# Graph layers on one core: three VectorE operands moved forward in order, and two pairs of column-sum products joined

## The chip, the core and the metric

The kernel runs on one core of a Trainium2 chip. The metric is the device time of one execution in microseconds (us); the time before is the median of three runs. One further execution was recorded by the hardware profiler, and everything about single instructions comes from that one. Engines are called TensorE (PE in the profile; PEld is its weight load), VectorE (DVE), ScalarE (ACT), GpSimd (POOL) and SyncE (SP, which issues transfers here). All data is fp32.

## The reference

For each of 16 graphs there are a feature matrix x (1024 nodes x 128) and an adjacency matrix adj (1024 x 1024). What matters of it:

```python
# first network, then a residual and a layer norm
degree = adj.sum(axis=-1)[:, :, None]
s = einsum('bid,bij->bjd', x, adj) / degree
x = layernorm(x + relu(concat([x, s]) @ W.T + b))

# second network: four layers, then a residual and a layer norm
def layer(nodes, ws, bs, wd, bd, wn, bn, wu, bu):
    src = einsum('bjv,bij->biv', nodes @ ws + bs, adj / norm_of_rows(adj))
    dst = einsum('bjv,bji->biv', nodes @ wd + bd, adj / norm_of_columns(adj))
    own = nodes @ wn + bn
    return tanh(concat([src, own, dst]) @ wu + bu)
# layers three and four read earlier outputs beside the last one
```

So each graph needs the Euclidean norms of the rows and of the columns of adj, row sums (degrees), and two layer norms over 128 features.

## The kernel before

**Loop.** The program runs over the 16 graphs, `for b in range(B)`. Within a step it does layers one to four of the second network for graph b and, in the gaps of the other engines, prepares graph n = b + 1: it loads adj, takes sums and norms, scales rows and columns, runs the first network (`first_gnn`, between layers three and four) and its layer norm (during layer four). The layer norm that ends graph b - 1 is done during layer two of graph b. The source counts layers from 0: l = 0, 1, 2, 3 are layers one to four.

**Order.** The order on each engine is written by hand (`manual_schedule`): instructions stand on an engine as the Python code issues them. A layer's matrix products come from lists; `aggregate` walks them and calls `hooks[i]` ahead of the i-th product of the upper list. These hooks place the other engines' work, and the small products, among the large ones.

**Halves.** A product fills 64 of the 128 columns of the TensorE array, so two run at the same time, one for the upper and one for the lower 64 output rows (`flat_steps`, `in_turn`). TensorE takes its instructions in order, alternating between the halves. Each fp32 product stands in the trace as two records.

**A layer.** `messages` or, for layers three and four, `paired_messages` computes what nodes send: TensorE writes into PSUM banks (tag `pt`, four buffers used in turn), VectorE adds the bias and writes the tiles t. `message_sums` makes from them the operands of a seven-product scheme (in place of eight): S3 = X00 - X10, S1 = X10 + X11, S2 = S1 - X00, S4 = X01 - S2, each with a SRC and a DST part. On the other side stand combinations of the adjacency (T, Q). In layers three and four the nodes' own features go through the same scheme, with T2, T3, T4 made in `begin_paired`, `t3()` and `t4()`. `aggregate` then runs the products M1 to M4 and Z11 to Z21 and adds their results up through the tiles e0, e1 and e2; `m2_and_half_of_m3` (line 906) is one of those reads, and it issues the addition of line 908.

**Sums over partitions.** VectorE reduces along the free axis. What is left across partition groups is summed on TensorE by `sum_groups` (line 247): two products with the constant `fold`, one per half, 32 columns wide. Six such sums are taken per graph: `pc` in `inverses` (column norms, layer two), `pm` in `norm_centre` and `pv` in `norm_rstd` (mean and variance of the layer norm, once in layer two and once in layer four), and `rp` in `gather_inverses` (row factors, layer three). Powers of -0.5 are taken on GpSimd (lines 374 and 454).

The changed places, by lines of before: column sums 340 to 343, `inverses` 360 to 370, `row_inverses` and `gather_inverses` 376 to 389, `norm_sum` and `norm_centre` 423 to 439, `messages` and `message_sums` 684 to 712, `begin_paired` and `paired_messages` 714 to 823, `aggregate` from 906 on, and the hooks of layers two, three and four.

Of the kernel before, what the change touches and what calls it, by code (L numbers as in the profile page):

```python
# [8 lines left out]
F32 = mybir.dt.float32  # L9
# [5 lines left out]
P = 128  # L15
# [8 lines left out]
def adj_resnorm_kernel(ctx: ExitStack, tc: tile.TileContext, x, adj, w0, b0, layers, out):  # L24
# [118 lines left out]
    def message_seven(wm):  # L143
        return seven(wm, (wm, MSUMS), 2 * P, P)
# [94 lines left out]
    def small(name, shape=(K,)):  # L239
        return ps_s.tile([P, *shape], F32, tag="small", name=name)  # L240
# [6 lines left out]
    def sum_groups(out, y):  # L247

        for s in (slice(V, P), slice(V)):
            nc.tensor.matmul(out[s], fold, y, start=True, stop=True)  # L250
# [89 lines left out]
    def column_reduce(b, state, tr):  # L340
        part = two.tile([P, K], F32, tag="part", name=f"part{b}")
        nc.vector.reduce_sum(part, tr.rearrange("p (k r) -> p k r", r=C), axis=AX.X)
        state["part"] = part
# [15 lines left out]

    def inverses(b, state, first=0):  # L360

        cols = state["cols"]
        pc = small(f"pc{b}")
        sum_groups(pc, state["part"])
        own = one.tile([P, NH, G, BPH], F32, tag="own", name=f"own{b}")
        nc.vector.tensor_mul(own, pc.rearrange("p (h g k) -> p h g k", h=NH, g=G),
                             group[:, None, :, None].to_broadcast([P, NH, G, BPH]))
        nc.vector.reduce_sum(cols[:, NB:2 * NB].rearrange("p (h k) -> p h k", h=NH),
                             own.rearrange("p h g k -> p h k g"), axis=AX.X)
        root_inverses(cols, state["inv"], slice(first, 2 * NB))  # L370
# [4 lines left out]

    def row_inverses(b, inv):

        spread = one.tile([P, NH, G, BPH], F32, tag="own", name=f"sp{b}")
        nc.vector.tensor_mul(spread, inv[:, :NB].rearrange("p (h k) -> p h k", h=NH)[:, :, None, :]
                             .to_broadcast([P, NH, G, BPH]),  # L380
                             group[:, None, :, None].to_broadcast([P, NH, G, BPH]))
        return spread
# [39 lines left out]

    def norm_sum(ys, ks, name, xs=None):

        if xs is not None:
            nc.vector.tensor_add(ys[:, ks], ys[:, ks], xs[:, ks])
        s = two.tile([P, ks.stop - ks.start], F32, tag="part", name=f"s{name}")
        nc.vector.reduce_sum(s, ys[:, ks], axis=AX.X)
        return s

    def norm_centre(ys, s, ks, name):
        n = ks.stop - ks.start
        pm = small(f"pm{name}")
        sum_groups(pm[:, :n], s)
        nc.vector.scalar_tensor_tensor(ys[:, ks], pm[:, :n, None].to_broadcast([P, n, C]), -1.0 / D,
                                       ys[:, ks], op0=ALU.mult, op1=ALU.add)
        sq = two.tile([P, n, C], F32, tag="sq", name=f"sq{name}")
        nc.scalar.activation(sq, ys[:, ks], AF.Square)
        return sq
# [244 lines left out]
    def messages(b, l, feats, wm, between={}, with_sums=True):  # L684


        nch = CHUNKS[l]
        t = [one.tile([P, NJ, 2, 2, V], F32, tag=f"t{j}", name=f"t{l + 1}_{b}_{j}") for j in range(2)]
        for n, g in enumerate((2, 3, 0, 1)):
            pt = ps_t.tile([P, 2, 2 * P], F32, tag="pt", name=f"pt{l + 1}_{b}_{g}")  # L690
            for q in range(2):
                i = 2 * g + q
                for k, (f, c) in enumerate(feats):
                    by_halves(pt[:, q], f[:, i * P:(i + 1) * P], wm[:, 1 + c], k == 0, k == nch - 1)
            j, o = divmod(2 * g, NJ)
            nc.vector.tensor_add(t[j][:, o:o + 2].rearrange("p k a v c -> p k (a v c)"), pt,
                                 wm[:, 0][:, None, :].to_broadcast([P, 2, 2 * P]))
            if n in between:
                between[n]()
        return message_sums(b, l, t) if with_sums else t  # L700

    def message_sums(b, l, t):

        S = {i: one.tile([P, NJ, 2, V], F32, tag=f"S{i}", name=f"S{i}_{l + 1}_{b}") for i in (2, 3, 4)}
        X = {(v, j): t[j][:, :, :, v] for v in range(2) for j in range(2)}
        S[1] = X[1, 0]
        for part in (DST, SRC):
            nc.vector.tensor_sub(S[3][:, :, part], X[0, 0][:, :, part], X[1, 0][:, :, part])
        nc.vector.tensor_add(S[1], X[1, 0], X[1, 1])  # L709
        nc.vector.tensor_sub(S[2], S[1], X[0, 0])  # L710
        nc.vector.tensor_sub(S[4], X[0, 1], S[2])
        return X, S

    def begin_paired(b, l, first, second, etag):

        e12 = one.tile([P, 2, HW], F32, tag=etag, name=f"e12_{l}_{b}")
        y = {(j, h): f[:, half(h)] for j, f in enumerate((first, second)) for h in range(NH)}
        w = {"e12": e12, "y": y, "T2": e12[:, 1], "T4": e12[:, 0]}
        nc.vector.tensor_sub(w["T2"], y[1, 1], y[0, 1])
        return w  # L720

    def paired_messages(b, l, w, wm, rest=None, between={}):

        t = [one.tile([P, NJ, 2, 2, V], F32, tag=f"t{j}", name=f"t{l + 1}_{b}_{j}") for j in range(2)]
        X = {(v, j): t[j][:, :, :, v] for v in range(2) for j in range(2)}
        y, s, T2, T4 = w["y"], message_seven(wm), w["T2"], w["T4"]
        T3 = w["e0"] = one.tile([P, HW], F32, tag="e0", name=f"e0_{l}_{b}")
        o = own_seven(l, wm)
# [41 lines left out]
        if l == 2:  # L770
            at(0)
            m4 = into(bank(4), (y[0, 1], s["S1"]))
            nc.scalar.copy(X[1, 1], parts(m4))
            m1 = into(bank(1), (y[0, 0], s["w00"]))
            add_bias((0, 0), parts(m1), 0)
            t3()
            t4()
# [15 lines left out]
        else:  # L793
# [25 lines left out]
            at(4)  # L819
        XS = message_sums(b, l, t)  # L820
        if l == 2:
            at(3)
        return XS

# [27 lines left out]
    def aggregate(b, l, feats, msgs, wm, a, at, T, Q, fT, etag, hooks={}, pieces=1, w=None):  # L852
# [50 lines left out]
        def m3_half():  # L903
            nc.scalar.copy(e1[high], Dk[low])

        def m2_and_half_of_m3():
            m2_read()
            nc.vector.tensor_add(e0[high], e0[high], e1[high])

# [24 lines left out]
        elif l == 1:  # L934
# [15 lines left out]

            events = {10: first_reads, 14: m4_read, 18: m2_and_half_of_m3, 22: last_reads}
        else:
# [303 lines left out]
    at = [transposed(0, h) for h in range(NH)]  # L1256
    back = None

    for b in range(B):
# [142 lines left out]
        else:  # L1404
# [3 lines left out]
            if nxt:  # L1408
                sums_of_next = {0: sums_of(4, 5), 1: sums_of(of=FIRST, add=(4, 5)), 2: sums_of(6, 7),
                                8: sums_of(add=(6, 7)), 9: lambda: column_sums(n, st), 15: sums_of(of=(4,)),  # L1410
                                18: sums_of(of=(5,)), 20: lambda: inverses(n, st), 21: sums_of(of=(6,)),
                                24: sums_of(of=(7,))}

            def begin1(w=w, nm=nm):
                norm_spread(w["ys"], f4, KS)
                w["s"] = norm_sum(w["ys"], KS, nm, back)

            def centre1(w=w, nm=nm):
                w["sq"] = norm_centre(w["ys"], w["s"], KS, nm)
                if nxt:  # L1420
                    w["xs"] = load_spread(n)

            def squares1(w=w, nm=nm):
# [4 lines left out]

            hooks = alongside(sums_of_next, {2: begin1, 16: centre1, 19: squares1, 26: rstd1})
        hooks = alongside(hooks, {3: weights2})  # L1430
# [39 lines left out]
        def factors_of_rows(w=w):  # L1470
            w["spread"] = row_inverses(n, st["inv"])

        def factors_gathered(w=w):
            w["rinv"] = gather_inverses(n, w["spread"])

# [14 lines left out]
        if nxt:  # L1490
            scales = [lambda: scale(0, 1), lambda: scale(NJ, 1), lambda: scale(0, 0), lambda: scale(NJ, 0)]
            if b == 0:
                between = {1: inverses3, 2: factors}
                hooks = {1: load_xn, 5: factors_of_rows, 7: start3, 18: factors_gathered,
                         **dict(zip((10, 12, 14, 16), scales))}
                quarters_at = (20, 22, 25)
            else:
                between = {0: factors, 3: end1_and_load}
                hooks = {2: factors_of_rows, **dict(zip((4, 5, 7, 9), scales)), 10: factors_gathered, 16: start3}
                quarters_at = (12, 14, 25)  # L1500
            hooks |= dict(zip(quarters_at, (quarter1, x_sums, quarter2)))
# [11 lines left out]
        if nxt:  # L1513
            yT = first_gnn(n, w["X"], w["xT"], quarters(a2), w["T2"], w["dinv"])
            rinv = w["rinv"]

# [4 lines left out]
        if nxt:  # L1521
# [19 lines left out]

            def sum0(w=w):
                w["s"] = norm_sum(w["ys"], KS, nm)

            def centre0(w=w):
                w["sq"] = norm_centre(w["ys"], w["s"], KS, nm)

# [141 lines left out]
```

## Time and profile before

| what | value |
|---|---|
| median of three runs | 2396.12 us (2395.91 to 2396.41) |
| the profiled execution, its own time | 2395.86 us |
| its span, first to last instruction | 2394.1 us |
| mean granted TensorE clock | 0.999 of full speed |
| records of TensorE products with 32 columns | 368, that is 92 sums: pm 30, pv 30, pc 16, rp 16 |
| one graph, from pv of layer two to the next (552.07 to 698.51 us) | 146.44 us |
| VectorE busy in such a stretch (702.1 to 848.6 us) | 131.85 us |
| ScalarE busy in it | 61.27 us |

The page gives busy time by engine, the share of the span in 40 slices, the chain of work that ended last, and groups of equal instructions by line. A line such as `L1003 PE MATMUL m<-a,t 128*64 128x512 f32` is an instruction of line 1003 of the kernel that writes tile m from tiles a and t, with 64 columns of the array and 512 columns of data. In a timeline a row has its start, how long it took, what it is, how many equal ones were merged (x), and in brackets the idle time ahead of it. Ends of TensorE products are modelled; starts are recorded.

### The profile page before, as it was taken

The page shows a single profiled execution, that of the slowest core. Times are in us where ns is not written, and L with a number is a line of the kernel's source. Part 1 is how long each engine was busy: PE and PEld are TensorE (multiplying, and loading weights), DVE is VectorE, ACT ScalarE, POOL GpSimd, SP SyncE. Part 2 cuts the span into 40 slices and gives each one's busy share as a digit, 9 for nine tenths or more (in the row PEclk, how much of TensorE's full clock was granted, in tenths as well). Part 3 has the DMA queues.
Part 4 walks back from the last instruction along what each step waited for, and adds up shares of the span by engine and source line. Part 5 has one row for each costly group of instructions (what it writes and reads, how often), then busy time and mean ns, then how long its engine had stood idle before and what let it go on. Part 6 is the DMA issues. An engine that isn't in the chain of part 4 may idle for free.

```text
span 2394.1 us, 39329 instructions
## 1 busy us (share of the span) xinstructions
PE 2377.4 (99%) x15289; PEld 1279.6 (53%) x15289; DVE 2092.6 (87%) x2817; ACT 980.8 (41%) x1845; POOL 275.8 (12%) x103
## 2 busy tenths in 40 slices
PE   8999999999999999999999999999999999999998
PEld 4444564645556455554655546456464554645555
DVE  6998888999889989889988889888898988998954
ACT  5425345253343524435244452434525344352322
POOL 4101111001111011110111110111100111101110
PEclk9999999999999999999999999999999999999999
DMA  9527244262533627335272442634427253362400
GB/s 205 124 75 147 69 115 90 70 148 57 135 78 81 138 48 157 61 97 115 55 163 55 108 97 71 147 69 110 91 70 151 57 133 76 80 141 48 100 22 22
DMA packets 363387, 232.03 MB, mean 97 GB/s; under 512 B 150353, under 2 KB 334306, under 8 KB 363202
## 3 DMA queue, kind: packets, MB, share of 16 engines
q1 hardware_dynamic: 362386, 227.03, 42.5%
q0 software_dynamic: 816, 2.49, 0.4%
q8 instruction: 121, 1.98, 0.4%
q14 instruction: 64, 0.52, 0.1%
HBM read 209.59 MB, written 19.84 MB: 96 GB/s over the span
## 4 chain that ended last, share of the span: by engine, by line
PE 92%; DVE 1%; issue 0%; POOLq 0%; ACT 0%; DVEq 0%
PE m L1003 40%; PE z L1003 28%; PE pt L245 9%; PE pt_z L245 5%; PE m_f L581 5%; PE z_f L581 2%; PE pw L245 2%; PE m3s L1003 1%; PE pt_p L245 1%; DVE t L752 0%; PE pv L250 0%; PE pm L250 0%; DVE f L534 0%; PE rp L250 0%; DVE t L758 0%
## 5 line engine op out<-in xcount | busy, mean ns | idle before, releaser
L1003 PE MATMUL m<-a,t 128*64 128x512 f32 x1008 | 434.7, 593 | 0.2 <-DVE t L709 0.2
L1003 PE MATMUL m<-at,t 128*64 128x512 f32 x1008 | 418.6, 592 | 0.0
L1003 PE MATMUL m<-Q,S 128*64 128x512 f32 x880 | 394.0, 593 | 0.0
L1003 PE MATMUL m<-T,S 128*64 128x512 f32 (+1 forms) x1040 | 393.6, 573 | 0.0
L454 POOL TENSOR_TENSOR rs<-ve,mhalf 128x32 f32<-128x32 f32 x30 | 191.9, 6396 | 988.4 <-DVE ve L452 988.4
L1003 PE MATMUL z<-at,t 128*64 128x512 f32 x504 | 229.2, 592 | 0.0
L1003 PE MATMUL z<-at,S 128*64 128x512 f32 x504 | 228.3, 593 | 0.0
L1003 PE MATMUL z<-a,S 128*64 128x512 f32 x504 | 228.2, 593 | 0.0
L1003 PE MATMUL z<-a,t 128*64 128x512 f32 x504 | 227.2, 593 | 0.0
L1003 PE MATMUL z<-Q,t 128*64 128x512 f32 x504 | 227.0, 593 | 0.0
L1003 PEld LDWEIGHTS m<-T,S 128*64 128x64 f32 x1040 | 131.3, 137 | 129.5 <-issue 127.6
L1003 PEld LDWEIGHTS m<-Q,S 128*64 128x64 f32 x880 | 118.2, 137 | 150.4 <-issue 143.0
L1003 PEld LDWEIGHTS m<-at,t 128*64 128x64 f32 x1008 | 131.6, 137 | 110.7 <-issue 109.4
L1003 PEld LDWEIGHTS m<-a,t 128*64 128x64 f32 x1008 | 132.0, 137 | 109.8 <-issue 101.0
L1003 PE MATMUL z<-T,t 128*64 128x512 f32 x384 | 172.8, 592 | 0.0
L882 ACT COPY e<-m 64x512 f32<-64x512 f32 x63 | 36.7, 582 | 327.4 <-PE m L1003 327.0
L374 POOL TENSOR_TENSOR inv<-cols,mhalf 128x16 f32<-128x16 f32 (+1 forms) x17 | 46.8, 2751 | 1033.3 <-DVE cols L373 1033.3
L412 DVE TENSOR_TENSOR a<-a,cinv 128x512 f32<-128x512 f32 x250 | 155.6, 696 | 0.8 <-DMA xn<-in_x_dram 0.8
L320 ACT ACTIVATE sq<-a 128x1024 f32<-128x1024 f32 x120 | 125.9, 1050 | 37.0 <-DVE acc L327 23.1
L245 PE MATMUL pt<-wm,f1T 128*64 128x128 f32 (+1 forms) x1536 | 134.3, 309 | 1.2 <-ACT f1T L1021 1.2
L245 PEld LDWEIGHTS pt<-wm,f1T 128*64 128x64 f32 x1536 | 109.1, 137 | 34.6 <-issue 12.3
L315 ACT ACTIVATE a<-a 128x1024 f32<-128x1024 f32 x120 | 125.3, 1045 | 0.4
(309 smaller groups left out, 5023.3 us busy)
## 6 DMA issues: line engine op xcount, KB each, us to landing
a<-in_adj_dram SPq DMA_DIRECT2D x120, 512.0 KB
rows<-in_adj_dram SPq DMA_DIRECT2D x480, 64.0 KB
a<-in_adj_dram SPq DMA_DIRECT2D x240, 128.0 KB
wm<-wsave SPq DMA_DIRECT2D x32, 704.0 KB
wm<-wsave SPq DMA_DIRECT2D x31, 320.0 KB
xn<-in_x_dram SPq DMA_DIRECT2D x124, 64.0 KB
xs<-in_x_dram SPq DMA_DIRECT2D x60, 128.0 KB
cinv<-dr SPq DMA_DIRECT2D x30, 256.0 KB
```

The lines of the kernel that those rows point to most:

```text
L245: nc.tensor.matmul(out[s], x[:, s], y, start=start, stop=stop)
L315: nc.scalar.activation(a[:, i, :], a[:, i, :], AF.Copy, accum_out=degree)
L320: nc.scalar.activation(sq, a[:, i, :], AF.Square, accum_out=state["cols"][:, i:i + 1])
L374: nc.gpsimd.tensor_tensor(inv[:, s], cols[:, s], mhalf[:, s], ALU.pow)
L412: engine.tensor_mul(a[:, i, s], a[:, i, s], cinv[:, s])
L454: nc.gpsimd.tensor_tensor(rstd, ve, mhalf[:, :n], ALU.pow)
L581: nc.tensor.matmul(o, x_, y_, start=start, stop=stop)
L882: nc.scalar.copy(e0[high], A[high])
L1003: nc.tensor.matmul(o, x, y_, start=start, stop=stop)
```

## The change

It has five parts.

1. `column_reduce` and `norm_sum` of layer two write the two halves of one tile of 64 columns (tag `both`). One `sum_groups` sums both; `inverses` and `norm_centre` read their part of the result. The centring moves from hook 16 to hook 19, the squares from 19 to 20, and `inverses`, which stood at 20, follows the centring. The four transfers of `load_spread` move along.
2. The row factors' partial values are kept until layer four and summed with the mean of that norm. `gather_inverses` is no longer called for graphs 1 to 15; ScalarE, not VectorE, copies the factors out of PSUM.
3. Layer one of graphs 1 to 15 takes its messages in the order 0, 1, 2, 3 instead of 2, 3, 0, 1, and makes S3 after the second of them.
4. Layer three makes T3 ahead of all its products, not after the addition of M1's bias. T3 and T4 swap buffers. Layer four makes S3 and S1 one part at a time, DST first.
5. In layer two the addition of line 908 gets an event of its own, at product 20 instead of 18.

```diff
-        part = two.tile([P, K], F32, tag="part", name=f"part{b}")
-        nc.vector.reduce_sum(part, tr.rearrange("p (k r) -> p k r", r=C), axis=AX.X)
+        part = state["part"] if "part" in state else one.tile([P, 2 * K], F32, tag="both", name=f"part{b}")
+        nc.vector.reduce_sum(part[:, :K], tr.rearrange("p (k r) -> p k r", r=C), axis=AX.X)
...
+    def sums_of_both(both, name):
+        pm = small(name, [2 * K])
+        sum_groups(pm, both)
+        return pm[:, :K], pm[:, K:]
...
-        for n, g in enumerate((2, 3, 0, 1)):
+        S, X = sums_tiles(b, l, t) if with_sums else (None, None)
+        for n, g in enumerate((2, 3, 0, 1) if l or b == 0 else range(NQ)):
...
+            if l == 0 and with_sums and n == 1:
+                sums_3(X, S)
...
+    def sums_3(X, S, parts=(DST, SRC)):
+        for part in parts:
+            nc.vector.tensor_sub(S[3][:, :, part], X[0, 0][:, :, part], X[1, 0][:, :, part])
+
+    def message_sums(X, S, parts=()):
+
         S[1] = X[1, 0]
-        for part in (DST, SRC):
-            nc.vector.tensor_sub(S[3][:, :, part], X[0, 0][:, :, part], X[1, 0][:, :, part])
-        nc.vector.tensor_add(S[1], X[1, 0], X[1, 1])
+        for part in parts:
+            sums_3(X, S, (part,))
+            nc.vector.tensor_add(S[1][:, :, part], X[1, 0][:, :, part], X[1, 1][:, :, part])
+        if not parts:
+            nc.vector.tensor_add(S[1], X[1, 0], X[1, 1])
...
-        T3 = w["e0"] = one.tile([P, HW], F32, tag="e0", name=f"e0_{l}_{b}")
+        e0 = w["e0"] = one.tile([P, HW], F32, tag="e0", name=f"e0_{l}_{b}")
+        T3, T4 = (w["e12"][:, 0], e0) if l == 2 else (e0, w["e12"][:, 0])
...
         if l == 2:
             at(0)
+            t3()
             m4 = into(bank(4), (y[0, 1], s["S1"]))
...
             add_bias((0, 0), parts(m1), 0)
-            t3()
             t4()
...
-            events = {10: first_reads, 14: m4_read, 18: m2_and_half_of_m3, 22: last_reads}
+            events = {10: first_reads, 14: m4_read, 18: m2_read, 20: half_of_m3, 22: last_reads}
...
             def centre1(w=w, nm=nm):
-                w["sq"] = norm_centre(w["ys"], w["s"], KS, nm)
+                pc, pm = sums_of_both(st["part"], f"pc{n}") if nxt else (None, None)
+                w["sq"] = norm_centre(w["ys"], w["s"], KS, nm, pm)
                 if nxt:
                     w["xs"] = load_spread(n)
+                    inverses(n, st, pc=pc)
...
-            hooks = alongside(sums_of_next, {2: begin1, 16: centre1, 19: squares1, 26: rstd1})
+            hooks = alongside(sums_of_next, {2: begin1, 19: centre1, 20: squares1, 26: rstd1})
...
-            def centre0(w=w):
-                w["sq"] = norm_centre(w["ys"], w["s"], KS, nm)
+            def centre0(w=w, both=both):
+                nonlocal rinv
+                pr, pm = sums_of_both(both, f"pm{nm}")
+                rinv = one.tile([P, K], F32, tag="rinv", name=f"rinv{n}")
+                nc.scalar.copy(rinv, pr)
+                w["sq"] = norm_centre(w["ys"], w["s"], KS, nm, pm)
```

More of the change, by code (lines that the diff above doesn't have):

```diff
@@ L358, in factor_bank, with inverses @@
         return pb
-    def inverses(b, state, first=0):
+    def inverses(b, state, first=0, pc=None):
         cols = state["cols"]
-        pc = small(f"pc{b}")
-        sum_groups(pc, state["part"])
-        own = one.tile([P, NH, G, BPH], F32, tag="own", name=f"own{b}")
+        if pc is None:
+            pc = small(f"pc{b}")
+            sum_groups(pc, state["part"][:, :K])
+        own = two.tile([P, NH, G, BPH], F32, tag="part", name=f"own{b}")
         nc.vector.tensor_mul(own, pc.rearrange("p (h g k) -> p h g k", h=NH, g=G),
@@ L374, in root_inverses, with row_inverses @@
         nc.gpsimd.tensor_tensor(inv[:, s], cols[:, s], mhalf[:, s], ALU.pow)
-    def row_inverses(b, inv):
-        spread = one.tile([P, NH, G, BPH], F32, tag="own", name=f"sp{b}")
+    def row_inverses(b, inv, both=None):
+        spread = two.tile([P, K], F32, tag="part", name=f"sp{b}") if both is None else both[:, :K]
+        spread = spread.rearrange("p (h g k) -> p h g k", h=NH, g=G)
         nc.vector.tensor_mul(spread, inv[:, :NB].rearrange("p (h k) -> p h k", h=NH)[:, :, None, :]
@@ L421, in norm_spread, with norm_sum, norm_centre @@
         nc.vector.transpose(ys[:, ks].rearrange("p k f -> p (k f)"), fT[:, ks.start * C:ks.stop * C])
-    def norm_sum(ys, ks, name, xs=None):
+    def norm_sum(ys, ks, name, xs=None, both=None):
         if xs is not None:
             nc.vector.tensor_add(ys[:, ks], ys[:, ks], xs[:, ks])
-        s = two.tile([P, ks.stop - ks.start], F32, tag="part", name=f"s{name}")
+        s = two.tile([P, ks.stop - ks.start], F32, tag="part", name=f"s{name}") if both is None else both[:, K:]
         nc.vector.reduce_sum(s, ys[:, ks], axis=AX.X)
         return s
-    def norm_centre(ys, s, ks, name):
+    def sums_of_both(both, name):
+        pm = small(name, [2 * K])
+        sum_groups(pm, both)
+        return pm[:, :K], pm[:, K:]
+    def norm_centre(ys, s, ks, name, pm=None):
         n = ks.stop - ks.start
-        pm = small(f"pm{name}")
-        sum_groups(pm[:, :n], s)
+        if pm is None:
+            pm = small(f"pm{name}")
+            sum_groups(pm[:, :n], s)
         nc.vector.scalar_tensor_tensor(ys[:, ks], pm[:, :n, None].to_broadcast([P, n, C]), -1.0 / D,
@@ L699, in messages, with sums_tiles @@
                 between[n]()
-        return message_sums(b, l, t) if with_sums else t
-    def message_sums(b, l, t):
-        S = {i: one.tile([P, NJ, 2, V], F32, tag=f"S{i}", name=f"S{i}_{l + 1}_{b}") for i in (2, 3, 4)}
-        X = {(v, j): t[j][:, :, :, v] for v in range(2) for j in range(2)}
-        S[1] = X[1, 0]
-        for part in (DST, SRC):
-            nc.vector.tensor_sub(S[3][:, :, part], X[0, 0][:, :, part], X[1, 0][:, :, part])
-        nc.vector.tensor_add(S[1], X[1, 0], X[1, 1])
+            if l == 0 and with_sums and n == 1:
+                sums_3(X, S)
+        if not with_sums:
+            return t
+        if l:
+            sums_3(X, S)
+        return message_sums(X, S)
+    def sums_tiles(b, l, t):
+        S = {i: one.tile([P, NJ, 2, V], F32, tag=f"S{i}", name=f"S{i}_{l + 1}_{b}") for i in (2, 3, 4)}
+        return S, {(v, j): t[j][:, :, :, v] for v in range(2) for j in range(2)}
+    def sums_3(X, S, parts=(DST, SRC)):
+        for part in parts:
+            nc.vector.tensor_sub(S[3][:, :, part], X[0, 0][:, :, part], X[1, 0][:, :, part])
+    def message_sums(X, S, parts=()):
+        S[1] = X[1, 0]
+        for part in parts:
[3 more added lines that the diff above has]
+            nc.vector.tensor_add(S[1], X[1, 0], X[1, 1])
         nc.vector.tensor_sub(S[2], S[1], X[0, 0])
@@ L717, in begin_paired @@
         y = {(j, h): f[:, half(h)] for j, f in enumerate((first, second)) for h in range(NH)}
-        w = {"e12": e12, "y": y, "T2": e12[:, 1], "T4": e12[:, 0]}
+        w = {"e12": e12, "y": y, "T2": e12[:, 1]}
         nc.vector.tensor_sub(w["T2"], y[1, 1], y[0, 1])
@@ L725, in paired_messages @@
         X = {(v, j): t[j][:, :, :, v] for v in range(2) for j in range(2)}
-        y, s, T2, T4 = w["y"], message_seven(wm), w["T2"], w["T4"]
-        T3 = w["e0"] = one.tile([P, HW], F32, tag="e0", name=f"e0_{l}_{b}")
+        y, s, T2 = w["y"], message_seven(wm), w["T2"]
+        e0 = w["e0"] = one.tile([P, HW], F32, tag="e0", name=f"e0_{l}_{b}")
+        T3, T4 = (w["e12"][:, 0], e0) if l == 2 else (e0, w["e12"][:, 0])
         o = own_seven(l, wm)
@@ L819, in paired_messages @@
             at(4)
-        XS = message_sums(b, l, t)
+        S, _ = sums_tiles(b, l, t)
         if l == 2:
+            sums_3(X, S)
+            XS = message_sums(X, S)
             at(3)
+        else:
+            XS = message_sums(X, S, (DST, SRC))
         return XS
@@ L904, in m3_half, with half_of_m3 @@
             nc.scalar.copy(e1[high], Dk[low])
+        def half_of_m3():
+            nc.vector.tensor_add(e0[high], e0[high], e1[high])
         def m2_and_half_of_m3():
             m2_read()
-            nc.vector.tensor_add(e0[high], e0[high], e1[high])
+            half_of_m3()
         def last_reads():
@@ L1256, in adj_resnorm_kernel @@
     at = [transposed(0, h) for h in range(NH)]
-    back = None
+    back = rinv = None
     for b in range(B):
@@ L1410, in adj_resnorm_kernel @@
                                 8: sums_of(add=(6, 7)), 9: lambda: column_sums(n, st), 15: sums_of(of=(4,)),
-                                18: sums_of(of=(5,)), 20: lambda: inverses(n, st), 21: sums_of(of=(6,)),
-                                24: sums_of(of=(7,))}
+                                18: sums_of(of=(5,)), 21: sums_of(of=(6,)), 24: sums_of(of=(7,))}
+                st["part"] = one.tile([P, 2 * K], F32, tag="both", name=f"part{n}")
             def begin1(w=w, nm=nm):
                 norm_spread(w["ys"], f4, KS)
-                w["s"] = norm_sum(w["ys"], KS, nm, back)
+                w["s"] = norm_sum(w["ys"], KS, nm, back, st.get("part"))
             def centre1(w=w, nm=nm):
-                w["sq"] = norm_centre(w["ys"], w["s"], KS, nm)
+                pc, pm = sums_of_both(st["part"], f"pc{n}") if nxt else (None, None)
+                w["sq"] = norm_centre(w["ys"], w["s"], KS, nm, pm)
                 if nxt:
                     w["xs"] = load_spread(n)
+                    inverses(n, st, pc=pc)
             def squares1(w=w, nm=nm):
@@ L1470, in factors_of_rows @@
         def factors_of_rows(w=w):
-            w["spread"] = row_inverses(n, st["inv"])
-        def factors_gathered(w=w):
-            w["rinv"] = gather_inverses(n, w["spread"])
+            w["both"] = one.tile([P, 2 * K], F32, tag="both", name=f"both{n}")
+            row_inverses(n, st["inv"], w["both"])
         def scale(i, h):
@@ L1493, in adj_resnorm_kernel @@
                 between = {1: inverses3, 2: factors}
-                hooks = {1: load_xn, 5: factors_of_rows, 7: start3, 18: factors_gathered,
+                hooks = {1: load_xn, 5: factors_of_rows, 7: start3,
                          **dict(zip((10, 12, 14, 16), scales))}
@@ L1498, in adj_resnorm_kernel @@
                 between = {0: factors, 3: end1_and_load}
-                hooks = {2: factors_of_rows, **dict(zip((4, 5, 7, 9), scales)), 10: factors_gathered, 16: start3}
+                hooks = {2: factors_of_rows, **dict(zip((4, 5, 7, 9), scales)), 16: start3}
                 quarters_at = (12, 14, 25)
@@ L1514, in adj_resnorm_kernel @@
             yT = first_gnn(n, w["X"], w["xT"], quarters(a2), w["T2"], w["dinv"])
-            rinv = w["rinv"]
+            both = w["both"]
         feats = [(x1T, 2), (f1, 1), (f23, 0)]
@@ L1540, in spread0, with sum0 @@
                 half_of_rows(2, 0, "xa")
-            def sum0(w=w):
-                w["s"] = norm_sum(w["ys"], KS, nm)
-            def centre0(w=w):
-                w["sq"] = norm_centre(w["ys"], w["s"], KS, nm)
+            def sum0(w=w, both=both):
+                w["s"] = norm_sum(w["ys"], KS, nm, None, both)
+            def centre0(w=w, both=both):
[4 more added lines that the diff above has]
+                w["sq"] = norm_centre(w["ys"], w["s"], KS, nm, pm)
             def squares0(w=w):
```

## The prediction

> **What bounds the kernel.** I read the page's busy line, its clock row and its chain first, then TensorE's waits, then TensorE's and VectorE's timelines side by side in the element b = 4 (702 to 849 us), where the loop has settled.
>
> ```profile
> span 2394.1 us, 39329 instructions
> PE 2377.4 (99%) x15289; PEld 1279.6 (53%) x15289; DVE 2092.6 (87%) x2817; ACT 980.8 (41%) x1845; POOL 275.8 (12%) x103
> PEclk9999999999999999999999999999999999999999
> PE 92%; DVE 1%; issue 0%; POOLq 0%; ACT 0%; DVEq 0%
> ```
>
> TensorE is busy from end to end at full clock, so time is won only by taking products away or by closing gaps between them. The waits look nearly empty; the three lines that touch this change all belong to the first element (b = 0):
>
> ```profile
> PE pt L245 <- DVE e L719: 1.2, 1, 1.2
> PE pt L245 <- DVE e L761: 1.0, 1, 1.0
> PE m L1003 <- DVE t L709: 0.2, 1, 0.2
> ```
>
> But that view counts idleness only after a product's modelled end. A 512-column pass is shown as 593 ns while passes of one half start 0.429 us apart (692.38, 692.81), so a late start up to 0.16 us is never seen, nor one that stops only one half of the array. I therefore go by starts. Two passes make a product, two halves run side by side, and one product of 512 columns per half (0.858 us) is called a slot. One element lasts 146.44 us (pv of 552.07 to pv of 698.51), and all settled elements repeat to 0.01 us. What is won in one is won 14 times (b = 1 to 14).
>
> **Part 1, shared products.** TensorE's timeline around a column sum, where one half reads m, the other z:
>
> ```profile
> 692.81 0.59 PE L1003 MATMUL m<-Q,S 128*64 128x512 f32 x1
> 693.24 0.19 PE L250 MATMUL pc<-part,fold 128*64 128x32 f32 x1
> 693.27 0.22 PE L250 MATMUL pc<-part,fold 128*64 128x32 f32 x1
> 693.33 0.62 PE L1003 MATMUL m<-Q,S 128*64 128x512 f32 x1
> 693.79 1.02 PE L1003 MATMUL m<-Q,S 128*64 128x512 f32 x2
> 694.65 0.59 PE L1003 MATMUL m<-Q,S 128*64 128x512 f32 x1
> ```
>
> From 692.81 to 694.65 lie four passes of m: 1.84 us where 4 x 0.429 = 1.72 were due. A 32-column product costs 0.12 us per half. The change takes 29 away: pc into pm for n = 2 to 15 (14), rp into pm for n = 1 to 15 (15). The survivor has 64 columns. Its price has two ends. By the rows, a 128-column pass takes 0.107 us where one half runs alone (702.17, 702.28, 702.39), hence 64 columns 0.053 against 0.027, twice: 0.053 us more, and 0.067 saved. The Trainium skill (TensorEngine Tiling (Array Packing), Instruction Overhead) says a matmul has some 60 cycles of overhead and one with a free dimension of 1 takes as long as one of 60: then 64 columns are all but free and 0.12 is saved. The rows show between: the passes of pc start 0.03 apart, as 32 columns should, but m follows the second by 0.06, so some floor is there and its half of the added columns is hidden. I take 0.095: 29 x 0.095 = **2.8 us** (1.9 to 3.5).
>
> The shared products wait for the later operand. In layer two it moves to slot 19, about 692.3, and the column sums end at 691.41 (L342 at 690.19 for 1.22): 0.7 us in hand with dispatch of 0.15. The instructions ahead of L342 on VectorE stay. Norm one is centred three slots later, but L435 and L366 to L373 then follow L890 without the 1.10 us that L908 waits today for ScalarE, since half_of_m3 goes behind them. L444 would end near 696.5, and pv comes at 698.5. On SP the four loads of xs are issued three slots later, with none passed; L417 uses them at 729.77. GpSimd's power for inv starts sooner. These cost nothing.
>
> In layer four the mean's product is there already; sp is ready 40 us before. VectorE loses a 178 ns copy (L388), ScalarE gains one. Here a rule speaks against the change: the Trainium skill (PSUM — Partial Sum Buffer, PSUM bank collisions) says two engines must not access one bank and quadrant at the same time, two readers included. The rows of before agree only in having one reader of pm; the changed program does make the centring (L435) wait for ScalarE's copy. pm ends at 758.47; with 0.1 us of dispatch and a copy of about 0.20 (estimate: 282 ns at 128 columns, 378 at 256 extrapolated to 32) the centring starts near 759.0, not 758.74: 0.25 us later on VectorE. ScalarE is idle there for 7.09 us before L438, so no queue comes on top. Without the rule it is 0, with it 0.25, and I carry 0.25 on.
>
> **Part 2, three operands.** (a) Layer four, S1:
>
> ```profile
> 764.30 1.11 PE L1003 MATMUL m<-e,wx 128*64 128x512 f32 x4
> 765.16 0.25 PE L250 MATMUL pv<-v,fold 128*64 128x32 f32 x2
> 765.25 0.25 PE L250 MATMUL pv<-v,fold 128*64 128x32 f32 x2
> 765.61 1.54 PE L1003 MATMUL m<-a,t 128*64 128x512 f32 x6
> ```
>
> ```profile
> 763.99 0.75 DVE L708 TENSOR_TENSOR S<-t 128x256 f32<-128x256 f32 x2
> 764.77 0.69 DVE L709 TENSOR_TENSOR t<-t,t 128x512 f32<-128x512 f32 x1
> 765.50 0.69 DVE L710 TENSOR_TENSOR S<-t 128x512 f32<-128x512 f32 x1
> ```
>
> M4 of the lower half reads S1, which ends at 765.46; it starts at 765.61 where pv would let it start at 765.34. The lower half loses 0.27 us. With S3 and S1 made by parts (0.42 each, 0.04 between), the DST part of S1 ends 0.88 us after S3 begins; with the 0.25 of above, 765.12, dispatched 765.27: in time by 0.07. The price: S1 takes 2 x 0.42 for 0.69 and S2 ends at about 766.7 instead of 766.19; M2 asks for it at 766.99. 0.15 us is in hand; gone, each 0.1 more costs 0.1 on the upper half.
>
> (b) Layer three, T3, same view of VectorE:
>
> ```profile
> 704.46 0.69 DVE L758 TENSOR_TENSOR t<-pt,wm 128x512 f32<-128x512 f32 x1 [0.50 <-PE pt L245]
> 705.07 0.68 DVE L761 TENSOR_TENSOR e<-e,f1T 128x512 f32<-128x512 f32 x1
> 705.67 0.69 DVE L764 TENSOR_TENSOR e<-f23T,e 128x512 f32<-128x512 f32 x1
> ```
>
> T3 ends at 705.75 and its first product starts at 705.90; the upper half was free at 705.63 and loses 0.27. Moved in front of L758, T3 fills VectorE's idle half microsecond before 704.46, L758 slips 0.2, T4 ends earlier than today. Next in line is the bank of m4, freed by ScalarE (L773, 704.06 for 0.57): before 705.6, so free. T3 and T4 swap buffers because e0 is still read by the tanh.
>
> (c) Layer one, S3: its DST part ends near 795.20, M3 starts at 795.35 where 795.27 was due: 0.08 on the lower half. In the new order S3 comes two adds earlier, but the third and fourth bank are freed 0.75 us later and M1 needs the third: 795.17 with dispatch against 794.91. That looks worse; but VectorE's chain there hangs on the lower half (transposes at 780.06 start when layer four is done with at1), so it moves up with the 0.27 of (a). I count (c) as 0 to 0.08.
>
> The sum is not 0.27 + 0.27 + 0.08. Upper loses 0.27 at (b), lower 0.35 at (a) and (c); in the records neither leads the other by more than a pass, so each hides the other's loss, and only all together give 0.27 to 0.35 per element. Allowing for thin margins I take 0.28: 14 x 0.28 = **3.9 us** (1.4 to 4.9).
>
> b = 0: T3 would be ready 0.9 us sooner, but the bank of m4 is freed at 116.25 (L773), so M3 starts at 116.40 for 116.64: 0.25. S1 gains there, S2 loses as much. b = 15: 0.1. Together **0.35** (0 to 0.8).
>
> **Sum:** 2.8 + 3.9 + 0.35 = 7.05 us from the profiled execution's own 2395.86 (span 2394.1 and 1.8 around it): 2388.8. The median shown is 0.26 higher, so **2389.1 us**. No change is within 0.2%, 4.8 us.
>
> **Rivals.** The margins give way (chance 0.20): ScalarE's copy and the split S1 make M2 wait for S2 in place of M4 for S1, and M1 for its bank. For it: margins of 0.07 and 0.15. Against: they are worked with full dispatch times. Only the products remain: 2.8 to 3.5, 2393. More than forecast (0.20): the 60-cycle rule holds and all gaps close: 3.5 + 4.9 + 0.8 = 9.2, 2386.9. Slower (0.05): the shared product of layer two stands in TensorE's queue for an operand of VectorE's long chain of squares. From 0.7 us late on, each microsecond stops both halves, 14 times; beyond 1.5 us late it eats the gain and 4.8 more: 2401 and up. Against it: pc waits at slot 20 today and shows no wait at all.
>
> **Chances.** Forecast 0.55, most of it faster; with the 0.20 above, 0.74 faster; 0.20 the same; 0.06 slower. The range goes from 2386, the larger rival, to 2394.5, half of the smaller gain.
>
> **What shows it.** 116 records of 64 columns, 136 of 32 left; period near 145.97; M4 right behind pv; the first T3 product without a gap. A gap before M2 in layer four, or before the 64-column product of layer two, would make me wrong.

## The result, and the profile after

| | before | after |
|---|---|---|
| median | 2396.17 us (2395.91 to 2396.77, 6 runs) | 2387.07 us (2386.61 to 2387.74, 6 runs) |
| ratio, 95% interval | | 0.9959 (0.9949 to 0.9969) |
| the profiled execution, its own time | 2395.86 us | 2386.61 us |
| its span | 2394.1 us | 2384.8 us |
| period: one settled graph to the next | 146.44 us | 145.84 us |

The change saves 9.1 us; 7.05 were forecast. The page of after, its span, its busy line, its clock row and its chain by engine:

```profile
span 2384.8 us, 39082 instructions
PE 2370.0 (99%) x15173; PEld 1602.9 (67%) x15173; DVE 2093.8 (88%) x2818; ACT 981.7 (41%) x1860; POOL 282.5 (12%) x103
PEclk9999999999999999999999999999999999999999
PE 94%; DVE 2%; DMA 2%; SPq 1%; issue 0%; ACT 0%; POOLq 0%; DVEq 0%
```

Nothing has taken TensorE's place: still 99% busy, at full clock. It issues 116 product records fewer, and VectorE has one instruction more. So the gain must be found in TensorE's starts, as the forecast said, and there it is nearly all in the settled loop: 14 graphs at 0.60 us less are 8.4 us of the 9.1. The other 0.7 lies at the two ends. How it divides there cannot be read from two executions: the first interval between starts of the first network's products went from 149.13 to 147.39 us, but it is 147.94 in e7_wide too, whose edit changes no period, and what stands ahead of that interval is 1.7 us longer there (148.90 for 147.24).

**The shared product.** Groups by form of after, the shared products alone (columns: line, engine, operation, tiles, array columns, shape, count, busy us, mean ns, idle before):

```profile
L250 PE MATMUL pm<-both,fold 128*64 128x64 f32 x60 | 7.9, 222 | 0.0
L250 PE MATMUL pc<-part,fold 128*64 128x64 f32 x56 | 7.5, 220 | 0.0
```

The count announced is there: 60 + 56 = 116 records of 64 columns. Of 32 columns 136 are left (120 pv, 8 pc, 4 pm, 4 rp). TensorE's timeline of after around the shared product of layer two (start, length, instruction, number merged):

```profile
689.41 0.59 PE L1035 MATMUL m<-Q,S 128*64 128x512 f32 x1
...
689.84 0.28 PE L250 MATMUL pc<-part,fold 128*64 128x64 f32 x2
689.96 0.59 PE L1035 MATMUL m<-Q,S 128*64 128x512 f32 x1
...
690.39 0.59 PE L1035 MATMUL m<-Q,S 128*64 128x512 f32 x1
```

Follow the half that reads m: 689.41, 689.96, 690.39. The second distance is a bare pass, 0.43; the first is 0.55, a pass and 0.12 for the 64-column product. That is what a 32-column product cost before. No wait stands in front of it: VectorE finished the column sums at 688.78 (L342 of after, 687.56 for 1.22), 1.06 us ahead.

**The operands.** VectorE's timeline of after at the start of layer four:

```profile
761.16 0.41 DVE L724 TENSOR_TENSOR S<-t 128x256 f32<-128x256 f32 x1
761.61 0.42 DVE L731 TENSOR_TENSOR t<-t,t 128x256 f32<-128x256 f32 x1
...
762.86 0.69 DVE L734 TENSOR_TENSOR S<-t 128x512 f32<-128x512 f32 x1
```

and TensorE's of the same kernel:

```profile
762.13 0.25 PE L250 MATMUL pv<-v,fold 128*64 128x32 f32 x2
762.22 0.62 PE L1035 MATMUL m<-a,t 128*64 128x512 f32 x1
762.39 0.25 PE L250 MATMUL pv<-v,fold 128*64 128x32 f32 x2
762.48 1.91 PE L1035 MATMUL m<-a,t 128*64 128x512 f32 x7
763.97 1.02 PE L1035 MATMUL m<-T,S 128*64 128x512 f32 x3
```

The DST part of S1 ends at 762.03 and both m follow their pv by 0.09: no half waits for S1 any more. S2 ends at 763.55, and M2, which runs on the upper half, begins at 763.97, 1.75 after M1 at 762.22: that is four passes of 0.429 and the 0.03 by which the first pass after a small product is longer, and no new gap.

### The profile page after: what moved, and what is told of

Its sections match the earlier page's. It is cut to its first block, busy times and chain, and to the rows that moved or that the text cites. A ratio compares the mean times of both kernels' runs of the same rounds, so it can differ in the third digit from the quotient of the medians.

```text
span 2384.8 us, 39082 instructions
## 1 busy us (share of the span) xinstructions
PE 2370.0 (99%) x15173; PEld 1602.9 (67%) x15173; DVE 2093.8 (88%) x2818; ACT 981.7 (41%) x1860; POOL 282.5 (12%) x103
## 4 chain that ended last, share of the span: by engine, by line
PE 94%; DVE 2%; DMA 2%; SPq 1%; issue 0%; ACT 0%; POOLq 0%; DVEq 0%
PE m L1035 35%; PE z L1035 34%; PE pt L245 9%; PE pt_z L245 5%; PE m_f L589 4%; PE z_f L589 3%; PE pw L245 2%; PE m3s L1035 1%; DMA Q<-in_adj_dram 1%; PE pt_p L245 1%; DMA wm<-in_L_gnn_ws_dram 1%; DVE acc L329 0%; DVE at L661 0%; DMA a<-in_adj_dram 0%; DVE a L414 0%
## 5 line engine op out<-in xcount | busy, mean ns | idle before, releaser
L1035 PE MATMUL m<-T,S 128*64 128x512 f32 (+1 forms) x1040 | 398.5, 572 | 0.0
L1035 PEld LDWEIGHTS m<-T,S 128*64 128x64 f32 x1040 | 141.8, 137 | 77.1 <-issue 4.9
L1035 PEld LDWEIGHTS m<-at,t 128*64 128x64 f32 x1008 | 138.1, 137 | 77.6 <-issue 4.4
L375 POOL TENSOR_TENSOR inv<-cols,mhalf 128x16 f32<-128x16 f32 (+1 forms) x17 | 52.9, 3109 | 986.2 <-DVE cols L374 986.2
L245 PEld LDWEIGHTS pt<-wm,f1T 128*64 128x64 f32 x1536 | 115.8, 137 | 23.0 <-ACT f1T L1053 6.0
```

Source lines behind the costliest of these rows:

```text
L245: nc.tensor.matmul(out[s], x[:, s], y, start=start, stop=stop)
L375: nc.gpsimd.tensor_tensor(inv[:, s], cols[:, s], mhalf[:, s], ALU.pow)
L1035: nc.tensor.matmul(o, x, y_, start=start, stop=stop)
```

## The experiments

The period is the usual distance between settled graphs in a trace. It repeats to 0.01 us from graph to graph (three single graphs of e9_copy and e11_one_sum, 0.04 to 0.19 longer, are left out) and so tells apart what medians of 2390 us cannot. "Before" and "after" name the kernel that an edit starts from.

### The two parts apart

e1_merge is after with S1, S3 and T3 left as in before: the shared products alone, with the moved hooks and the moved event of line 908 that go with them.

```diff
-        T3, T4 = (w["e12"][:, 0], e0) if l == 2 else (e0, w["e12"][:, 0])
+        T3, T4 = e0, w["e12"][:, 0]
...
-            XS = message_sums(X, S, (DST, SRC))
+            sums_3(X, S)
+            XS = message_sums(X, S)
```

> The changed kernel without its three operands: only the shared products stay. If a product of 64 columns costs as much as one of 32 (0.12 us saved per product, 29 of them), it is 3.5 us faster than before and one graph takes 146.44 - 0.24 = 146.20 us. If the added columns are paid for in full (0.067 saved), 1.9 us and 146.31 us. The price taken in the prediction (0.095) would give 2.8 us and 146.25 us.

e2_operands is before with the three operands made as in after.

```diff
-        T3 = w["e0"] = one.tile([P, HW], F32, tag="e0", name=f"e0_{l}_{b}")
+        e0 = w["e0"] = one.tile([P, HW], F32, tag="e0", name=f"e0_{l}_{b}")
+        T3, T4 = (w["e12"][:, 0], e0) if l == 2 else (e0, w["e12"][:, 0])
...
+            if l == 3:
+                nc.vector.tensor_add(S[1][:, :, part], X[1, 0][:, :, part], X[1, 1][:, :, part])
...
-        for n, g in enumerate((2, 3, 0, 1)):
+        for n, g in enumerate((2, 3, 0, 1) if S3 is None else range(NQ)):
```

> Only the three operands made sooner, on the kernel before; products as before. The prediction's figure is 0.28 us per graph, 146.16 us and 4.3 us in all with the first graph; its upper end is 0.35, 146.09 us and 5.3 us. What the result leaves for the operands if a shared product saves 0.12 is 0.36 per graph.

| kernel | median, us | ratio (95%) | period, us | against before |
|---|---|---|---|---|
| e1_merge | 2393.42 | 0.9991 (0.9984 to 0.9998) | 146.227 | -0.212 |
| e2_operands | 2390.4 | 0.9976 (0.9967 to 0.9985) | 146.073 | -0.366 |

The operands carry more than the products, and each part works without the other. Together they make 0.578 of the 0.60; where the other 0.02 is, is shown under the small products.

### Each operand alone

e3_s1 makes only S1 of layer four by parts:

```diff
             nc.vector.tensor_sub(S[3][:, :, part], X[0, 0][:, :, part], X[1, 0][:, :, part])
-        nc.vector.tensor_add(S[1], X[1, 0], X[1, 1])
+            if l == 3:
+                nc.vector.tensor_add(S[1][:, :, part], X[1, 0][:, :, part], X[1, 1][:, :, part])
+        if l != 3:
+            nc.vector.tensor_add(S[1], X[1, 0], X[1, 1])
```

> Only S1 of layer four by parts, on the kernel before. Theory of the halves (each half hides the other's loss): the lower half keeps 0.08 and the upper its 0.27 at T3, so only 0.08 per graph is won, 146.36 us. Rival (each gap costs the mean over the two halves, whatever the other gaps do): 0.14 per graph, 146.30 us.

e4_t3 only makes T3 of layer three sooner:

```diff
+        T3, T4 = (w["e12"][:, 0], e0) if l == 2 else (e0, w["e12"][:, 0])
...
             at(0)
+            t3()
             m4 = into(bank(4), (y[0, 1], s["S1"]))
...
-            t3()
             t4()
```

> Only T3 of layer three made sooner, on the kernel before. Theory of the halves: the lower half still loses 0.35 per graph and sets the time, so nothing is won, 146.44 us; the first graph alone may give 0.25 us. Rival (the mean over the halves): 0.14 per graph, 146.30 us, 2 us in all.

e5_s1_t3 does both:

```diff
+        T3, T4 = (w["e12"][:, 0], e0) if l == 2 else (e0, w["e12"][:, 0])
...
+            if l == 3:
+                nc.vector.tensor_add(S[1][:, :, part], X[1, 0][:, :, part], X[1, 1][:, :, part])
```

> S1 by parts and T3 sooner together, on the kernel before. New theory, after S1 alone gave 0.27 per graph and T3 alone nothing: the lower half alone sets the time, and a loss on the upper half is hidden as long as it is no longer than the lead that the upper half has when the stage begins. Then T3 adds nothing to S1: 146.17 us per graph. If T3's 0.27 comes out once S1's loss is gone, it is below 146.0.

e6_s3 only changes layer one:

```diff
-        for n, g in enumerate((2, 3, 0, 1)):
+        for n, g in enumerate((2, 3, 0, 1) if S3 is None else range(NQ)):
...
+            if S3 is not None and n == 1:
+                for part in (DST, SRC):
+                    nc.vector.tensor_sub(S3[:, :, part], X[0, 0][:, :, part], X[1, 0][:, :, part])
```

> Only layer one's S3 sooner, in the order 0, 1, 2, 3, on the kernel before. If the lower half sets the time, its 0.08 is won at once: 146.36 us per graph. If the bank freed 0.75 us later stops the upper half and through it the lower one, nothing or a loss: 146.44 to 146.55.

| kernel | median, us | ratio (95%) | period, us | against before |
|---|---|---|---|---|
| e3_s1 | 2391.99 | 0.9984 (0.9976 to 0.9991) | 146.167 | -0.272 |
| e4_t3 | 2396.11 | 1.0 (0.9992 to 1.0009) | 146.433 | -0.006 |
| e5_s1_t3 | 2391.82 | 0.9979 (0.9971 to 0.9987) | 146.167 | -0.272 |
| e6_s3 | 2394.86 | 0.9993 (0.9983 to 1.0003) | 146.344 | -0.095 |

0.272 + 0.006 + 0.095 = 0.373, and e2 gave 0.366: the three add up, and none needs another. S1 alone brings all of its 0.27, T3 none of its 0.27, whether S1's loss is there or not.

VectorE's timeline of e3_s1, whose rows answer to L708 to L710 in the forecast:

```profile
763.30 0.41 DVE L708 TENSOR_TENSOR S<-t 128x256 f32<-128x256 f32 x1
763.74 0.43 DVE L710 TENSOR_TENSOR t<-t,t 128x256 f32<-128x256 f32 x1
```

and TensorE's of the same kernel:

```profile
764.46 0.25 PE L250 MATMUL pv<-v,fold 128*64 128x32 f32 x2
764.55 0.62 PE L1006 MATMUL m<-a,t 128*64 128x512 f32 x1
764.55 0.25 PE L250 MATMUL pv<-v,fold 128*64 128x32 f32 x2
764.63 1.91 PE L1006 MATMUL m<-a,t 128*64 128x512 f32 x7
```

The first part of S1 ends at 764.17, and the second m starts 0.17 after the first pv where before it took 0.45 (765.16 to 765.61). 0.28 is won there, and 0.27 arrives in the period. In e6_s3, TensorE's timeline where layer one goes from z to its seven products:

```profile
795.28 0.59 PE L1009 MATMUL m<-a,t 128*64 128x512 f32 x1
795.64 0.59 PE L1009 MATMUL m<-T,S 128*64 128x512 f32 x1
...
796.07 0.59 PE L1009 MATMUL m<-T,S 128*64 128x512 f32 x1
```

and in before:

```profile
795.35 0.61 PE L1003 MATMUL m<-T,S 128*64 128x512 f32 x1
...
795.80 0.59 PE L1003 MATMUL m<-T,S 128*64 128x512 f32 x1
```

M3 (reading T, S) begins 0.43 after the z pass at 795.21, a bare pass, and its second pass follows by 0.43. In before the two distances are 0.51 (from the z pass at 794.84) and 0.45. The difference of 0.10 is what the period gives. M1, which the forecast feared to see wait for its bank, begins 0.43 after its z too (794.86 to 795.28).

### Why T3 costs nothing

In the trace of before, the starts at T3 read one by one, with the half told apart by their spacing of 0.109 us, are:

```text
upper: 705.409  705.518  ............. T3's product 705.897  706.006
lower: 705.569  705.678  705.787  705.897 (last pass of M2)  T3's product 706.027
```

The upper half stops from 705.63 to 705.90. The lower half is 0.38 behind it, does its last passes meanwhile, and comes to T3 at 706.01, when T3 is there. It loses 0.02 at most. To test that a lead of this size is the cover, e12_t3_late makes the loss larger than the lead:

```diff
-            t3()
             t4()
+            t3()
```

> The kernel before with the two additions T4 and T3 of layer three changed over, so that T3 ends about 0.6 us later (about 706.35 where it was 705.75) and the upper half, free at 705.63, loses about 0.88 us in place of 0.27. Theory one, the lead: the upper half begins layer three one pass (0.43 us) ahead of the lower, and a loss up to that lead costs nothing: 0.88 - 0.43 = 0.45 us per graph, period 146.9, time 2396.2 + 14 x 0.45 = 2402.5. Theory two: any loss of the upper half at this place is made up by later waits of the same half, whatever its size: period 146.44, time 2396.2. Theory three: once the wait is this long it stops both halves from the first tenth on, since TensorE takes its instructions in order: 0.6 us or more per graph, period 147.05, time 2404.7 or above.

Measured: 2404.33 us, ratio 1.0038 (1.0024 to 1.0052), period 146.992, 0.553 more. TensorE's timeline of e12_t3_late:

```profile
707.67 1.09 PE L245 MATMUL pt<-wm,e 128*64 128x128 f32 x13
709.09 1.09 PE L245 MATMUL pt<-wm,e 128*64 128x128 f32 x16 [0.33 <-DVE e L761]
```

and its waits, the line of T3 (total us, times, longest):

```profile
PE pt L245 <- DVE e L761: 4.9, 15, 0.3
```

A wait that before showed in one graph now shows in all 15. From the starts, the upper half was free at 708.22 and the lower at 708.60; both begin at 709.09. The upper loses 0.87, the lower 0.50, and 0.87 minus the lead of 0.38 is about that 0.50. The lower half's first pass behind the stop then takes 0.16 where 0.11 is bare, in all 15 graphs: 0.50 and 0.05 are the 0.55 that the period grew. The result lies between what the first theory expected (it took the lead as a whole pass, 0.43) and the third; that the upper half's stop was paid in full is excluded, since its growth of 0.60 is not reached and the period repeats to 0.01.

So TensorE's time here is set by the trailing half alone. A stop of the leading half is paid only where it is longer than the lead. Where the leading half spends the time that T3 made sooner gives it (it must wait somewhere else, since e4 and e5 have the same periods as their partners without T3) was not tried.

### The price of a small product

e7_wide lets the mean's and the variance's products of before read their 32 columns twice, so that they are 64 wide; the second copy is not used.

```diff
+        wide = out.rearrange("p (u k) -> p u k", u=2)
+        for s in (slice(V, P), slice(V)):
+            nc.tensor.matmul(wide[s], fold, y[:, None, :].to_broadcast([P, 2, K]), start=True, stop=True)
```

> The kernel before with pm and pv (four products of 32 columns per graph, counted as two per norm) widened to 64 columns, by reading the same 32 columns twice; the second copy is not used. If a product has a floor that hides the added columns, one graph stays at 146.44 us. If the added columns are paid for in full, 4 x 0.053 more: 146.65 us. The joined products alone saved 0.106 per product, that is 0.014 for the added columns: then 146.49.

e8_twice issues the variance's product a second time.

```diff
         sum_groups(pv[:, :n], v)
+        sum_groups(pv[:, :n], v)
```

> The kernel before with pv's product issued twice in a row (same result). If a product costs 0.12 us wherever it stands, two more per graph cost 0.24: 146.68 us. If the second one in a row costs only its own columns and the floor, 0.05 to 0.06 each: 146.55 us.

e7_wide took 2396.55 us, ratio 1.0 (0.999 to 1.001), period 146.44: four products a graph twice as wide, and nothing to see. e8_twice took 2398.2, ratio 1.0007 (0.9997 to 1.0017), period 146.557: 0.118 for two products more. That is 0.059 each only on paper, for the two do not stand alike. TensorE's timeline of e8_twice in layer four:

```profile
766.10 0.40 PE L250 MATMUL pv<-v,fold 128*64 128x32 f32 x7
766.30 0.62 PE L1004 MATMUL m<-a,t 128*64 128x512 f32 x1
766.33 0.22 PE L250 MATMUL pv<-v,fold 128*64 128x32 f32 x1
766.55 1.23 PE L1004 MATMUL m<-a,t 128*64 128x512 f32 x4
```

and in layer two:

```profile
845.92 0.59 PE L1004 MATMUL z<-at,t 128*64 128x512 f32 x1
...
846.55 0.62 PE L1004 MATMUL z<-a,t 128*64 128x512 f32 x1
```

where before has

```profile
844.98 0.59 PE L1003 MATMUL z<-at,t 128*64 128x512 f32 x1
...
845.49 0.62 PE L1003 MATMUL z<-a,t 128*64 128x512 f32 x1
```

In layer four the lower half's M4 begins 0.45 us after the first pv, as in before (765.16 to 765.61): it waits for S1 in any case, and the second product falls into that wait. In layer two no wait covers it: from the pass ahead of pv to the one behind it are 0.63 us, where before it was 0.51. So one of the two products is hidden, and the other costs 0.12, as much as a single one. The second expectation named the right period for a wrong reason.

The starts of one half, read one by one, show where the price lies (us from the first pass of the small product to its second, from there to the next large pass, and what that large pass takes beyond 0.429):

| columns | where | first pass | second pass | next large pass, extra | sum |
|---|---|---|---|---|---|
| 32 | pv of after | 0.029 | 0.058 | 0.030 | 0.117 |
| 64 | pc of after | 0.056 | 0.058 | 0.003 | 0.117 |
| 96 | pc of e11_one_sum | 0.082 | 0.083 | 0.000 | 0.165 |

A product has a floor of 0.117 us: the columns from 33 to 64 fall under it, those from 65 to 96 cost 0.048. The Trainium skill (TensorEngine Tiling (Array Packing), Instruction Overhead) has such a floor, at 60 columns; the runs agree that 64 cost no more than 32, and they alone show the 0.117.

So two products less a graph are 2 x 0.117 = 0.234, and e1_merge gave 0.212. The 0.02 is at S1. In the forecast's layer four, M4 of the lower half begins 0.452 us after the first pv in before and 0.473 in e1_merge (medians of 15 graphs), since ScalarE's copy of the factors is ahead of the centring and S1, which still ends late in e1, comes later by as much. In after S1 has time in hand and the 0.02 is no longer paid: 0.234 + 0.366 = 0.600.

### The copy on ScalarE, and T3 in the changed kernel

e9_copy is after with VectorE making the copy of the row factors, as in before:

```diff
-                nc.scalar.copy(rinv, pr)
+                nc.vector.tensor_copy(rinv, pr)
```

> The changed kernel with the row factors copied out of PSUM by VectorE again (128x32, in front of the centring). If the centring's wait for ScalarE's copy costs nothing that sets the end, one graph stays at 145.84 us. If the 0.25 us of the prediction eat into S1's margin of 0.07, the copy on VectorE (0.18 with no crossing of engines) brings it down by up to 0.1; if VectorE's own time counts, up by as much.

e10_no_t3 is after with T3 in its old place:

```diff
             at(0)
-            t3()
             m4 = into(bank(4), (y[0, 1], s["S1"]))
...
             add_bias((0, 0), parts(m1), 0)
+            t3()
             t4()
```

> The changed kernel with T3 back in its old place. Hidden loss of the upper half: 145.84 us per graph as in the changed kernel, perhaps up to 145.86, because shared products and operands measured apart give 0.578 of the 0.60; the first graph 0.3 to 0.7 us later. If T3 matters once all else is gone: 146.1.

e9_copy took 2386.77 us, ratio 0.9959 (0.9943 to 0.9975), e10_no_t3 2387.24, ratio 0.9963 (0.9948 to 0.9978); both have a period of 145.84, that of after. VectorE's timeline of after at the copy:

```profile
755.28 0.69 DVE L780 TENSOR_TENSOR t<-t 128x512 f32<-128x512 f32 x1
755.90 1.23 DVE L443 SCALAR_TENSOR_TENSOR y<-pm,y 128x1024 f32<-128x1024 f32 x1
```

ScalarE's of the same kernel:

```profile
755.68 0.19 ACT L1581 COPY rinv<-pm 128x32 f32<-128x32 f32 x1 [5.64 <-PE pm L250]
```

The copy ends at 755.87. The centring comes 0.62 after the addition ahead of it, where that distance is 0.60 in before: it is 0.01 to 0.02 late, and not 0.25, because VectorE was itself occupied until then. T3's new place shows only in the first graph. The waits of after, one line:

```profile
PE pt L245 <- ACT t L799: 0.6, 1, 0.6
```

and in its place in those of e10_no_t3:

```profile
PE pt L245 <- DVE e L786: 1.0, 1, 1.0
```

With T3 sooner, its wait of 1.0 us becomes a wait of 0.6 for the bank that ScalarE frees, as forecast. In the medians it is worth 0.17 us, less than these can tell.

### One product more taken away

If only the number of small products counts, mean and variance can share one as well. e11_one_sum squares before the centring and takes the variance as the mean of the squares less the square of the mean; mean, variance and the partner's sums stand in one product of 96 columns, so 30 products more are gone.

```diff
+        nc.vector.reduce_sum(both[:, K:2 * K], ys[:, ks], axis=AX.X)
+        sq = two.tile([P, K, C], F32, tag="sq", name=f"sq{name}")
+        nc.scalar.activation(sq, ys[:, ks], AF.Square)
...
-        pm = small(name, [2 * K])
+        pm = small(name, [3 * K])
...
-            hooks = alongside(sums_of_next, {2: begin1, 19: centre1, 20: squares1, 26: rstd1})
+            hooks = alongside(sums_of_next, {2: begin1, 10: squares1, 19: centre1})
```

> The changed kernel with mean and variance of each layer norm from one product of 96 columns (squares taken before centring, variance as mean of squares less square of mean), so that pv's own product goes too, 30 in all; VectorE gets three small instructions more per norm. If a product costs 0.106 us and added columns nothing (64 gave nothing), 0.21 per graph less: 145.63 us, 3 us in all, 2384. If columns beyond 64 are paid for, 0.027 each way: 145.68. If the longer chain makes a product wait, above 145.84.

It took 2383.73 us (2383.16 to 2384.45), ratio 0.9948 (0.9931 to 0.9965): the shortest time measured here, though the interval of this ratio overlaps that of after. The period is plainer: 145.70, 0.137 under after. Its groups by form:

```profile
L250 PE MATMUL pc<-part,fold 128*64 128x96 f32 x60 | 5.0, 246 | 0.0
L250 PE MATMUL pm<-both,fold 128*64 128x96 f32 x60 | 5.0, 246 | 0.0
```

Two products fewer a graph would give 0.234; the third block of 32 columns takes 2 x 0.048 back. 0.138 is left, which is what was measured.

## Why the prediction was right, and which of its terms were off

| term | forecast, us | measured, us |
|---|---|---|
| shared products | 29 x 0.095 = 2.8 | 29 x 0.117 = 3.4 |
| operands | 14 x 0.28 = 3.9 | 14 x 0.366 = 5.1 |
| first and last graph | 0.35 | 0.6, what is left of 9.1 |
| sum | 7.05 | 9.1 |

- **Bound and method.** Right. TensorE stays busy throughout, the waits view hardly moves, and the starts tell all of it.
- **Shared products.** Right in kind, small in size. The term that was off is the price of the 32 columns that the survivor gains: half was taken as visible, midway between the slope of the rows (0.067 saved) and the skill's floor (0.12 saved). The floor holds: e7 shows the added columns at nothing. Passes of 128 columns, from which the slope was taken, lie above it.
- **Margins of the shared product.** Right: 1.06 us in hand for the 0.7 counted, no wait.
- **ScalarE's copy ahead of the centring.** The order is as forecast: the centring starts after the copy has ended. (No run here lets both read the bank at once, so what that would cost is not shown.) The 0.25 is wrong: 0.02 or less, since the copy ran beside an addition of VectorE. The step left out what VectorE was doing meanwhile.
- **S1.** Right: 0.27 lost and 0.27 won, the margin 0.30 for the 0.07 counted (762.03 and 0.15 of dispatch against M4 of the lower half at 762.48), since the 0.25 of the copy fell away, and S2 did not become late.
- **S3.** A little above its upper end, 0.095 for 0 to 0.08: the longer first pass behind the stop, 0.02, was not counted. But it doesn't hang on S1, as was argued: e6_s3 has it alone, without M1 waiting for a bank.
- **T3.** The forecast failed in how the losses combine: "each hides the other's loss, and only all together give 0.27 to 0.35 per element". The 0.27 of the upper half was real but already covered by the 0.38 that the lower half is behind (shown by e4, e5, e10 and e12); a lead of less than a pass was enough, since the loss was smaller still; the lower half's losses are paid whole and add up. The number 0.28 came out near 0.366 because S1 and S3 belong to the half that counts. By that reasoning S1 alone should have given 0.08, as e3_s1's expectation says; it gave 0.272.
- **First graph.** Too small: 0.25 for T3 and nothing for S1. T3's wait fell from 0.99 to 0.64 us. At S1 in layer four the time from the lower half's last pass ahead of pv to its M4 fell from 2.00 to 1.40 (1.41 in e3_s1, which changes S1 alone), 0.60 where a settled graph wins 0.28 (0.79 to 0.52); the forecast had set a gain and a loss against each other there. The two, 0.35 and 0.32, are about the 0.6 that is left, though single executions differ by more at this end.
- **Rivals.** The time came out at the larger one, 2386.9, whose product price is right, but not for its reason that all three gaps close: closing T3's adds nothing to a settled graph. No margin gave way.

## What to carry to other kernels

Where two halves of the array run side by side, first find which one trails, and by how much: its stops are paid in full, those of the leading half only beyond the lead. A small product among large ones is paid by the piece, not by the column, up to a width that is cheaply measured by doubling it (64 columns here, with 0.117 us for the piece); join such products until it is reached, and beyond it reckon the columns against the piece. Test the price where no wait follows: where the half waits for an operand in any case, a product more is hidden, as in layer four of e8_twice. A wait added ahead of an instruction costs only what goes beyond the work its engine has anyway, so the engine's own row at that time has to stand in the sum.

## What the runs showed of the hardware beyond that

- A second small product right behind the first is no cheaper than the first. In e8_twice the four passes of 32 columns of one half and the large pass behind them start 0.03, 0.06, 0.06 and 0.06 us apart: only the first pass is as short as its columns, the others take what passes of 64 columns take in after (0.056 and 0.058). The first large pass behind the small ones is 0.030 us longer than a bare one after 32 columns and 0.003 longer after 64.
- The busy share of weight loads says nothing of the time here. after and e9_copy have the same period with 67% and 55%, before has 53%, and e11_one_sum, the shortest of all, 43%. What differs in the starts is how far the halves are shifted against each other. From 560 to 2100 us the mean shift between starts of 512-column passes is 0.17 us in after, 0.06 in e9_copy and before, and 0.01 in e11_one_sum, and in all fourteen traces a larger shift goes with a larger share, with exceptions only where two shifts differ by about 0.01 us. A weight load is shown as 0.137 us, so loads of the two halves that start closer than that overlap and count once; no run changed the shift alone to show that this is the cause.
